# A message-passing layer on one core: another order inside each step, node blocks in smaller parts, and a later, longer shrinking of the pipeline's lags

## The chip, the core and the metric

The kernel runs on one core of a Trainium2 chip. Time is device microseconds of one execution. The kernel before took 2609.36 us (median of three executions, 2591.1 to 2622.12). The engines are called by the profile's names: PE (TensorE, matrix products), ACT (ScalarE), DVE (VectorE), POOL (GpSimd, which here only issues gathers) and SP (SyncE, which here only issues plain transfers).

## What is computed

A graph has 12,500 nodes with 64 features (`x`) and 200,000 edges, sorted by destination. Cut to what matters:

```python
nodes = x[edges].reshape(E, 128)                       # source row and destination row
gates = (ssp(edge_attr @ We1 + be1) @ We2 + be2) * soft_cutoff(edge_weight1)
h = ssp(nodes @ Wn1 + bn1) @ Wn2 + bn2
messages = h * gates                                   # E x 64
message_sum = zeros_like(x).at[dst].add(messages)
new = x + ssp(message_sum @ Ws1 + bs1) @ Ws2 + bs2
out = layernorm(x + new)                               # over the 64 features, no scale or shift
```

`ssp(v)` is `log(1 + exp(v)) - log 2`, and `soft_cutoff(d)` is `1 - sigmoid(5 (d - 3.5))`. All data are float32.

## The kernel before

**Groups.** The edges are worked on in 391 groups of 512, each as four columns of 128 (`K = 4`). Because edges are sorted by destination, the 256 edges of each half of a group go to destinations in a window of 42 neighbouring nodes (`W`); what would fall outside is dealt with after the loop in a branch that these data don't take.

**A group's chain**, with the lines of the profile:

- `gather` (L176, POOL): four indirect transfers fetch the source rows into `xg`, 128 rows each. They are issued 19 groups ahead (`AHEAD = 20`); `xg` has 25 buffers. In every 32nd group one of the four is fetched row by row through SP instead (`fetch`, L191, `xr`).
- `load` (L197, L204, SP): the edge attributes `eT` and two windows of a table of destination rows that are already multiplied by their part of `Wn1` (`wns`).
- `onehot` (L209, DVE): a one-hot of each edge's place in its window, beside the source row in `xg`.
- `transposes` (L217, PE, into a `tx` bank) and `xcopy` (L222, ACT, to `xT`): source rows and one-hots turned, so that one product with `wns` gives source part plus destination part.
- `layer1_edge` (L226, L228) and `layer1_node` (L233): first layers of the edge and node networks into one PSUM tile `z` of two banks. The edge part fills half of the first bank, the node part the other half and half of the second.
- `exps` (L243), `logs` (L246) on ACT and `softplus` (L251) on DVE: the activation, to `s`.
- `layer2_edge` (L257, L260) and `layer2_node` (L265) into `gh`.
- `hcut` (L270) and `message` (L274) on DVE: times the cutoff, and times the gates.
- `scatter` (L278, PE): messages times one-hots, that is, the sums over the window ("Sums' product"). It goes into the free half of the second bank of `z`, or into a `tx` bank in the last groups.
- `window` (L287, DVE): adds the two halves' 64 x 42 sums to `sums` at a place read from a register, which is loaded ahead of each of them.

PSUM holds eight banks: two `z` tiles of two banks, two of `gh`, two of `tx`.

**Order.** Nothing is planned by a scheduler. The code inside `tc.manual_schedule()` is the order on every engine, and each engine works through its instructions in that order, with waits on semaphores for what it needs from others. Step `i` of the loop works on different groups at once: layer 1 of group `i + 1`, layer 2 of `i - 1`, Sums' product of `i - 3`, transposes of `i + 3`. On PE a step is: Sums, layer 2 of the edges, layer 1, transposes, layer 2 of the nodes. On DVE: softplus, windows, h, message, one-hot. From step `both = last - CATCH_UP` on (`CATCH_UP = 12`, `last = 390`) the lags are shorter: layer 2 of `i`, Sums of `i - 1`, transposes of `i + 2`; the step in between does two groups of layer 2, the next one three of Sums.

**Node blocks.** When the sums of a block of 512 nodes are complete, the last network and the layer norm of this block are done inside the loop (`node_block`), in five parts, one in each following step: product with `Ws1` (L306) and clamping (L314, L315); logarithm on ACT (L318, L319) and softplus (L322); second product (L327, L330), doubling of `x` and centring (L334 to L337); square (L341) and variance (L345); root (L350, L351), scaling (L356 to L359) and store (L360). The block's rows of `x` (`y`, L312) are loaded in the first part. `block_steps` fixes after which group a block counts as complete. The last two blocks have 256 nodes each (`HE`); they are done after the last group, interleaved with each other. A part with a product takes a `tx` bank.

**Before the loop** constants, indices and the table of destination rows are prepared, among them `ws2` and the row of biases `brow`, which is cut into three bfloat16 pieces that a product adds up again.

Of the kernel before, what the change touches and what calls it, by code (L numbers as in the profile page):

```python
# [31 lines left out]

# [19 lines left out]

P = 128
D = 64
HE = 256
# [9 lines left out]
CATCH_UP = 12  # L65
# [7 lines left out]
def node_blocks(N):  # L73

    rest = N - NB
    first = rest % NB
    assert rest > 0 and first % 2 == 0 and first <= HE
    sizes = ([first] if first else []) + [NB] * (rest // NB) + [HE, HE]
    return [(sum(sizes[:i]), n) for i, n in enumerate(sizes)]
# [18 lines left out]
def gnn_resnorm_kernel(ctx: ExitStack, tc: tile.TileContext, a: dict, out: bass.AP, E: int):  # L98
# [52 lines left out]
    half = const.tile([P, 1], F32, name="half")  # L151
    ones3 = const.tile([PIECES, HE], BF16, name="ones3")
# [78 lines left out]
    def layer1_node(g, h):  # L231
        zn = zs[g][:, h, HE * (1 - h) : HE * (2 - h)]
        nc.tensor.matmul(zn, wns[:, g % REST, h, :], xTs[g][:, h], start=True, stop=True, skip_group_check=True)  # L233
# [29 lines left out]
    def layer2_node(g, h):  # L263
        for t in range(2):
            nc.tensor.matmul(ghs[g][:, 1, 2 * t + h, :], ss[g][:, 1 + h, t, :], wn2, start=False,  # L265
                             stop=h == 1 and t == 1, skip_group_check=True)
# [14 lines left out]

    def window(g):
        for h in range(2):
            base = nc.values_load(base_i[0:1, 2 * g + h : 2 * g + h + 1], engines=[DVE], min_val=0, max_val=N - 1,
                                  skip_runtime_bounds_check_because="it was clamped to these bounds")
            part = sums[h * D : (h + 1) * D, bass.ds(base, W)]
            nc.vector.tensor_add(part, part, scs[g][h * D : (h + 1) * D, h * W : (h + 1) * W])  # L287

    def node_block(first, n, pool):
# [7 lines left out]
        def tile3(name):  # L297
            return pool.tile([P, 2, 2, D], F32, name=name, bufs=2)[:p, :nq]
# [11 lines left out]
        def clamp():  # L310
            t["y"] = tile3("y")
            nc.sync.dma_start(t["y"], x[rows, :].rearrange("(q p k) d -> p q k d", q=nq, k=2))  # L312
            t["l"], t["zb"] = (pool.tile([P, HE], F32, name=name, bufs=2) for name in ("l_s", "zb"))
# [19 lines left out]
        def center():  # L333
            nc.vector.scalar_tensor_tensor(t["y"], t["y"], 2.0, t["u"][:, :nq], OP.mult, OP.add)  # L334
            mean = small("mean")
            nc.vector.tensor_reduce(mean, t["y"], AX.X, OP.add)
            nc.vector.scalar_tensor_tensor(t["y"], mean.to_broadcast([p, nq, 2, D]), -1.0 / D, t["y"], OP.mult, OP.add)  # L337
# [5 lines left out]
        def variance():  # L343
            t["v"] = small("var")
            nc.vector.tensor_reduce(t["v"], t["y2"], AX.X, OP.add)  # L345
            nc.vector.tensor_scalar(t["v"], t["v"], 1.0 / D, EPS, OP.mult, OP.add)

        def root():
            t["r"] = small("rstd")
            nc.scalar.activation(t["r"], t["v"], AF.Ln)  # L350
            nc.scalar.activation(t["r"], t["r"], AF.Exp, scale=-0.5)  # L351

        def store():

            v, r = t["v"], t["r"]
# [3 lines left out]
            nc.vector.tensor_mul(t["y"], t["y"], r.to_broadcast([p, nq, 2, D]))  # L359
            nc.sync.dma_start(out[rows, :].rearrange("(q p k) d -> p q k d", q=nq, k=2), t["y"])  # L360

        def then(f, g):
            def both():
                f()
                g()
            return both

        return [(hidden, clamp), (None, then(logs, ssp)), (layer2, center), (None, then(square, variance)),
                (None, then(root, store))]

    def node_part(part):
        if part[0]:
            part[0](tx_tile())
        part[1]()

    with tc.manual_schedule():
# [4 lines left out]
        with tc.tile_pool(name="prep", bufs=1) as prep:  # L381
# [23 lines left out]
            nc.vector.memset(half, 0.5)  # L405
            nc.vector.memset(ones3, 1.0)
# [40 lines left out]
            nc.vector.tensor_add(brow[:, 1:3, :], brow[:, 1:3, :], ps[:1, : 2 * D].rearrange("o (i d) -> o i d", d=D))  # L447
# [293 lines left out]
```

## Time and profile before

| | |
|---|---|
| median of three executions | 2609.36 us |
| the profiled execution | 1999.2 us, of which span 1997.4 us |
| mean granted clock of TensorE in it | 0.986 |
| busy: PE / weight loads / POOL | 1881.8 / 1505.4 / 1474.1 us |
| busy: DVE / ACT | 1050.5 / 919.0 us |
| first and last gather issued | 3.3 / 1950.2 us |
| moved by DMA | 143.15 MB, mean 72 GB/s |

The profiled execution is shorter than the three timed ones. Everything that is read from the trace belongs to this one execution. In the profile "idle before, releaser" is the time that an engine stood still ahead of an instruction and what ended it; "issue" means that nothing in the trace was waited for. A float32 product is recorded as two matmuls.

### The profile page before, as it was taken

To read this page: it belongs to the slowest core of one execution; us is meant where nothing else is said; L and a number is where in the kernel's file an instruction comes from. 1 tells how busy PE (TensorE), PEld (TensorE's weight loads), DVE (VectorE), ACT (ScalarE), POOL (GpSimd) and SP (SyncE) were. 2 spreads that over 40 slices of the span, in tenths; PEclk is the share of its full clock that TensorE was granted. 3 is DMA by queue.
4 is the path that set the end of the run, shared out by engine and by line. 5 is a ranking of instruction groups with operands and counts; after the bars stand their busy time and mean duration, and the time that the engine had idled before them with its cause. 6 is when DMAs were issued, how large, how long until landed. Compare 5 with 4: busy or idle time off the path is not lost.

```text
span 1997.4 us, 42101 instructions
## 1 busy us (share of the span) xinstructions
PE 1881.8 (94%) x11378; PEld 1505.4 (75%) x11378; DVE 1050.5 (53%) x2752; ACT 919.0 (46%) x1322; POOL 1474.1 (74%) x1555
## 2 busy tenths in 40 slices
PE   4999999999999999999999999999999999999996
PEld 4888888887777777777777777777777877777775
DVE  4455555555544545545555555555554555555555
ACT  1344545454444444444444444444454554444433
POOL 7777777777777777777777777777777777777770
PEclk9999999999999999999999999999998999999988
DMA  8432222222223223232222322232222232223220
GB/s 231 140 68 68 66 69 68 67 67 69 66 68 69 58 66 69 62 70 61 63 68 64 69 65 64 68 69 69 68 65 68 64 71 68 68 71 68 68 61 25
DMA packets 171021, 143.15 MB, mean 72 GB/s; under 512 B 46507, under 2 KB 142947, under 8 KB 170778
## 3 DMA queue, kind: packets, MB, share of 16 engines
q1 hardware_dynamic: 119778, 87.95, 15.2%
q0 software_dynamic: 49632, 50.92, 14.2%
q8 instruction: 95, 1.56, 0.3%
q10 hardware_dynamic: 1368, 1.51, 0.3%
q14 instruction: 148, 1.21, 0.2%
HBM read 130.57 MB, written 9.63 MB: 70 GB/s over the span
## 4 chain that ended last, share of the span: by engine, by line
PE 58%; DMA 20%; POOL 7%; issue 6%; ACT 4%; DVE 3%; DVEq 1%; POOLq 0%; SPq 0%; ACTq 0%
DMA xg<-in_x,src_i 19%; PE gh L265 11%; PE z L233 9%; PE gh L260 8%; PE z L228 8%; POOL xg L176 7%; PE tx L217 6%; PE z L278 6%; PE gh L257 4%; PE z L226 3%; ACT u L246 2%; ACT u L243 2%; PE z L471 2%; DVE s L251 1%; DVE sums L287 1%
## 5 line engine op out<-in xcount | busy, mean ns | idle before, releaser
L176 POOL DMA_INDIRECT xg<-in_x,src_i x1551 | 1473.9, 950 | 476.8 <-issue 310.0
L251 DVE SCALAR_TENSOR_TENSOR s<-u,z 128x768 f32<-128x768 f32 x392 | 373.2, 952 | 842.6 <-ACT u L246 776.7
L243 ACT ACTIVATE u<-z 128x768 f32<-128x768 f32 x392 | 317.4, 810 | 975.8 <-PE z L233 975.8
L233 PE MATMUL z<-xT,wns 106*128 106x256 f32 x1564 | 410.0, 384 | 0.0
L265 PE MATMUL gh<-consts,s 128*128 128x64 f32 x3128 | 394.1, 269 | 0.0
L265 PEld LDWEIGHTS gh<-consts,s 128*128 128x128 f32 x3128 | 391.6, 196 | 0.1
L246 ACT ACTIVATE u<-u,one 128x768 f32<-128x768 f32 x392 | 366.1, 934 | 12.3
L217 PE MATMUL tx<-consts,xg 128*106 128x128 f32 x1552 | 283.5, 283 | 69.9 <-DMA xg<-in_x,src_i 63.9
L233 PEld LDWEIGHTS z<-xT,wns 106*128 106x128 f32 x1564 | 301.3, 193 | 44.4 <-issue 0.4
L217 PEld LDWEIGHTS tx<-consts,xg 128*106 128x106 f32 x1552 | 194.9, 133 | 164.9 <-DMA xg<-in_x,src_i 116.1
L260 PE MATMUL gh<-consts,s 128*128 128x128 f32 x1564 | 279.9, 301 | 0.0
L228 PE MATMUL z<-eT,consts 128*128 128x256 f32 x782 | 277.9, 437 | 0.0
L260 PEld LDWEIGHTS gh<-consts,s 128*128 128x128 f32 x1564 | 205.1, 191 | 89.0 <-issue 88.3
L278 PE MATMUL z<-xg,msg 128*128 128x84 f32 x1500 | 235.4, 279 | 0.0
L222 ACT COPY xT<-tx 106x512 f32<-106x512 f32 x391 | 221.6, 567 | 9.5 <-PE tx L217 9.1
L278 PEld LDWEIGHTS z<-xg,msg 128*128 128x128 f32 x1500 | 198.1, 192 | 0.0
L270 DVE TENSOR_TENSOR h<-gh,cut 128x256 f32<-128x256 f32 x391 | 166.0, 425 | 14.7 <-PE gh L265 2.2
L274 DVE TENSOR_TENSOR msg<-gh,h 128x256 f32<-128x256 f32 x391 | 166.0, 425 | 13.5
L228 PEld LDWEIGHTS z<-eT,consts 128*128 128x128 f32 x782 | 118.0, 190 | 47.6 <-issue 1.5
L287 DVE TENSOR_TENSOR sums<-sums,z 64x42 f32 x750 | 144.3, 192 | 13.0 <-issue 6.1
L257 PE MATMUL gh<-row,ones 3*128 3x512 bf16 x391 | 150.8, 386 | 0.0
L209 DVE TENSOR_TENSOR xg<-consts,rel 128x168 f32<-128x168 f32 x391 | 126.8, 325 | 1.1 <-issue 0.4
(79 smaller groups left out, 590.9 us busy)
## 6 DMA issues: line engine op xcount, KB each, us to landing
eT<-in_eT SPq DMA_DIRECT2D x391, 128.0 KB
xg<-in_x,src_i POOLq DMA_INDIRECT x1551
xr<-in_x SPq DMA_DIRECT2D x1536, 0.2 KB
wns<-table SPq DMA_DIRECT2D x782, 21.0 KB
table<-tb SPq DMA_DIRECT2D x14, 448.0 KB
sums<-in_xT SPq DMA_DIRECT2D x7, 455.0 KB
y<-in_x SPq DMA_DIRECT2D x23, 128.0 KB
out<-y SPq DMA_DIRECT2D x23, 128.0 KB
```

Of the source, the lines that this page charges most:

```text
L176: nc.gpsimd.indirect_dma_start(out=xg[:, k, :D], out_offset=None, in_=x, in_offset=bass.IndirectOffsetOnAxis(ap=src_i[:, g, k : k + 1], ax ...
L217: nc.tensor.transpose(tx[:, k, :], row, ident)
L222: nc.scalar.copy(xT, xTs[g])
L228: nc.tensor.matmul(zs[g][:, 0, :HE], we1.rearrange("a h d -> a (h d)"), eTs[g], start=False, stop=True, skip_group_check=True)
L233: nc.tensor.matmul(zn, wns[:, g % REST, h, :], xTs[g][:, h], start=True, stop=True, skip_group_check=True)
L243: nc.scalar.activation(us[g][:, part], z_of(g)[:, part], AF.Exp)
L246: nc.scalar.activation(us[g][:, part], us[g][:, part], AF.Ln, bias=one)
L251: nc.vector.scalar_tensor_tensor(ss[g].rearrange("p i t e -> p (i t e)")[:, part], us[g][:, part], BIG, z_of(g)[:, part], OP.min, OP.max)
L257: nc.tensor.matmul(gh, ones3[:, :P], row3.rearrange("q i k d -> q (i k d)"), start=True, stop=False, skip_group_check=True)
L260: nc.tensor.matmul(v[:, 0, t], ss[g][:, 0, t, :], we2, start=False, stop=False, skip_group_check=True)
L265: nc.tensor.matmul(ghs[g][:, 1, 2 * t + h, :], ss[g][:, 1 + h, t, :], wn2, start=False, stop=h == 1 and t == 1, skip_group_check=True)
L278: nc.tensor.matmul(sc, msgs[g][:, 2 * t : 2 * t + 2, :].rearrange("p h f -> p (h f)"), xgs[g][:, 2 * t : 2 * t + 2, D:DW], start=t == 0, s ...
```

## The change

- **Order in a step.** On PE: layer 2 of the edges, layer 1 of the edges, a node block's product if there is one, layer 1 of the nodes, then Sums' product into the same `z` tile, transposes, layer 2 of the nodes. Sums' product goes into `z` in all but the last groups, so that `tx` is left to transposes and node blocks. On DVE: h, message, windows, one-hot, softplus, node parts. The two window places of a group are loaded into registers at once.
- **Node blocks.** A block has eleven parts (`Part`). The load of `y` is issued when five more groups are missing (`PREPARE`), the other ten parts stand in the steps `BLOCK_STEPS` after completion, up to the twelfth; towards the end in three steps (`BRIEFLY`). The columns of `ws2` and of the bias are centred beforehand, so `y` alone is centred, and this before the second product. The constant of the root comes in as a bias (`eps`). The last block is one of 512 nodes.
- **Lags.** From `ends = last - 14` on Sums are two groups behind instead of three; transposes go from three groups ahead to two and then to one, each time after a step without transposes, and then stand first in a step. Layer 2's lag stays. The last group and what is still behind it is written out after the loop, with the windows' places loaded ahead.

The diff, cut to its core:

```diff
-CATCH_UP = 12
+CATCH_UP = 14
+PREPARE = 5
+BLOCK_STEPS = (1, 2, 3, 3, 4, 5, 6, 7, 8, 12)
+BRIEFLY = (1, 1, 1, 1, 2, 2, 2, 3, 3, 3)
...
-    rest = N - NB
-    first = rest % NB
-    sizes = ([first] if first else []) + [NB] * (rest // NB) + [HE, HE]
+    first = N % NB
+    sizes = ([first] if first else []) + [NB] * (N // NB)
...
+    def window_bases(g):
+        _, window_at[g] = nc.values_load_multi_w_load_instructions(
+            base_i[0:1, 2 * g : 2 * g + 2], engines=[DVE], min_val=0, max_val=N - 1,
...
-        return [(hidden, clamp), (None, then(logs, ssp)), (layer2, center), (None, then(square, variance)),
-                (None, then(root, store))]
+        return [Part(None, fetch), Part(hidden, clamp), Part(None, logs), Part(None, center), Part(None, ssp),
+                Part(layer2, add), Part(None, square), Part(None, variance), Part(None, root), Part(None, scale),
+                Part(None, store)]
...
+            nc.vector.tensor_reduce(mean[:, :2], ws2, AX.X, OP.add)
+            nc.vector.tensor_reduce(mean[:1, 2:], brow[:, 3, :], AX.X, OP.add)
+            nc.vector.scalar_tensor_tensor(ws2, mean[:, :2].to_broadcast([P, 2, D]), -1.0 / D, ws2, OP.mult, OP.add)
+            nc.vector.scalar_tensor_tensor(brow[:, 3, :], mean[:1, 2:].to_broadcast([1, D]), -1.0 / D, brow[:, 3, :],
...
+                groups = [i - 3] if i < ends else [i - 3, i - 2] if i == ends else [i - 2]
                 third[i] = [g for g in groups if g >= 0]
+                ahead[i] = [i + 3] if i < ends else [i + 2] if i == ends + 1 else [i + 1] if i > ends + 2 else []
...
+            for i in range(-3, last - 1):
+                now = parts.pop(i, [])
                 at(load, i + LOADS)
                 fetch(i)
                 if i > 0:
                     at(gather, i + AHEAD - 1)
+                early = i > ends
+                if early:
+                    for g in ahead[i]:
+                        transposes(g)
+                        xcopy(g)
+                at(layer2_edge, i - 1)
+                if i >= -1:
                     zs[i + 1] = z_tile()
+                    layer1_edge(i + 1)
+                    for part in now:
+                        if part.tensor:
+                            part.tensor(tx_tile())
+                    layer1_node(i + 1)
+                for n, g in enumerate(third[i]):
+                    scatter(g, zs[i + 1][:, 1, HE + 2 * W * n : HE + 2 * W * (n + 1)])
+                at(exps, i + 1)
+                at(logs, i + 1)
+                if not early:
+                    for g in ahead[i]:
+                        transposes(g)
+                        xcopy(g)
+                at(layer2_node, i - 1)
+                at(hcut, i - 1)
+                at(message, i - 1)
+                for g in third[i]:
                     window(g)
                 for g in ahead[i]:
                     at(onehot, g + 2)
+                at(softplus, i + 1)
+                for part in now:
+                    part.others()
...
+            begun.pop(2).others()
+            transposes(last)
+            xcopy(last)
+            layer2_edge(last - 2)
+            zs[last] = z_tile()
+            layer1_edge(last)
+            layer1_node(last)
+            for some in (edge, node):
+                exps(last, some)
+                logs(last, some)
+            for g in range(last - 3, last + 1):
+                window_bases(g)
+            softplus(last, edge)
+            layer2_node(last - 2)
+            scatter(last - 3, tx_tile()[:, : 2 * W])
...
+            scatter(last, tx_tile()[:, : 2 * W])
+            window(last)
+            for part in begun:
+                node_part(part)
```

## The prediction

> **What bounds the kernel now.** I read the page's busy line and the gather's row first, then the waits, then busy time by stage, and last the timeline of the steady stretch, of the turn into the end phase and of the end.
>
> ```profile
> PE 1881.8 (94%) x11378; PEld 1505.4 (75%) x11378; DVE 1050.5 (53%) x2752; ACT 919.0 (46%) x1322; POOL 1474.1 (74%) x1555
> L176 POOL DMA_INDIRECT xg<-in_x,src_i x1551 | 1473.9, 950 | 476.8 <-issue 310.0
> ```
>
> POOL looks less loaded than PE, but each of its 1551 gathers costs 0.95 us and then 0.30 us before the next: 1.25 x 1551 = 1939 us from 3.3 us on, so the last starts at 1950.2. A group of four gathers takes 5.0 us.
>
> ```profile
> PEld tx L217 <- DMA xg<-in_x,src_i: 116.1, 209, 1.5
> PE tx L217 <- DMA xg<-in_x,src_i: 63.9, 155, 1.3
> ```
> ```profile
> 200.00:400.00 200.00, 199.98 (x1272) 164.86 (x1271) 109.44 (x284) 101.48 (x142) 151.50 (x160) 1.00 0.29 68
> 1000.00:1200.00 200.00, 190.19 (x1156) 150.44 (x1155) 102.57 (x272) 93.67 (x133) 151.25 (x160) 0.99 0.29 67
> ```
>
> Columns: length, then busy time and count of PE, weight loads, DVE, ACT, POOL, then granted clock. Until about 400 us PE lives on the twenty groups gathered ahead and never idles; later its rate falls by 1156/1272 although it isn't slower: its transposes wait for gathers. So from 400 us POOL sets the pace, and PE has 5.0 - 4.41 = 0.6 us a group to spare. The 4.41 is the distance of two L233 (299.69 and 304.10 us) and splits by the starts between them: transposes L217 0.44, L265 0.84, L278 0.55, L257 0.32, L260 0.65, L226 0.20, L228 0.54, L233 0.87.
>
> The end is different.
>
> ```profile
> 1920.00:1925.00 5.00, 5.00 (x17) 3.25 (x17) 2.19 (x7) 1.25 (x2) 3.78 (x4) 0.54 0.27 66
> 1925.00:1930.00 5.00, 5.00 (x21) 4.45 (x21) 2.61 (x7) 1.79 (x4) 3.77 (x4) 0.50 0.29 61
> ```
> ```profile
> 1918.28 0.65 PE L278 MATMUL tx<-xg,msg 128*128 128x84 f32 x4 [0.92 <-DVE sums L287]
> 1919.85 0.65 PE L278 MATMUL tx<-xg,msg 128*128 128x84 f32 x4 [0.92 <-DVE sums L287]
> 1950.19 0.94 POOL L176 DMA_INDIRECT xg<-in_x,src_i  x1 [0.30 <-DMA xg<-in_x,src_i]
> 1968.77 0.62 PE L217 MATMUL tx<-consts,xg 128*106 128x128 f32 x4 [0.22 <-PE z L233]
> 1971.02 1.03 PE L233 MATMUL z<-xT,wns 106*128 106x256 f32 x4
> 1983.10 0.20 DVE L287 TENSOR_TENSOR sums<-sums,tx 64x42 f32 x1 [0.36 <-DVE sums L287]
> 1992.07 0.29 DVE L359 TENSOR_TENSOR y<-y,rstd 128x128 f32<-128x128 f32 x1
> ```
>
> At the turn (step 378) PE computes one second layer and two Sums products extra and twice stands 0.92 us, because three products share two tx banks. Then it runs at half clock for some 14 us. It ends 16 us behind POOL: the last gather lands near 1952.7, but the last group's transposes start at 1968.8. From there it is one chain: first layer to 1972.05, last window 1983.3, last scaling 1992.4, the store's 5.0 us, 1997.4.
>
> **What the Trainium skill says.** "TensorE: Matmul & The Clock Gate", Part 1 (the HAM clock gate): an idle window of about 3.4 us puts TensorE at half clock. The trace shows half clock with much shorter stalls ahead: after 0.17 and 0.63 us of gather waits at 1531 to 1533 us the clock is 0.50 until 1548.5, and again after the turn above. "DMA: Bandwidth & Descriptors", Anatomy of one DMA: a transfer costs some 2 us fixed, mostly the write receipt; here the chain has 2.46 us from a gather's issue to its landing. "PSUM — Partial Sum Buffer", Terms: two engines must not be on one bank at once. That is why, in the built order, the exponential now waits for the Sums product that stands behind layer 1 in its tile; no timing of it is in this trace.
>
> **The change part by part.** *Sums product behind layer 1, every group.* The counts of PE, ACT and POOL instructions per group stay. PE's order becomes L257, L260, L226, L228, L233, Sums, transposes, L265: the same terms, 4.41 us. Whether a neighbour hides more or less of a weight load isn't shown; between -0.02 and +0.02 us a group, I take 0. The exponential starts 0.55 us later, and DVE now does h, message, windows, one-hot and only then the softplus. Counted from the end of L233: Sums 0.55, transposes 0.44, L265 0.84 and its drain 0.17 give 2.0; DVE adds 0.42 + 0.45 + 0.42 + 0.33 + 0.95, so the softplus ends at 4.6. ACT's two passes end at about 2.5, earlier. L260 wants that softplus a group later, at 4.41 + 1.83 + 0.32 = 6.56. Cover 1.95 us: cost 0. Behind the waiting exponential stand only the logarithm and the xT copy, wanted two groups later.
>
> *Node blocks over twelve steps.* The same twelve DVE instructions for a block, in eleven parts (the input's load first); a step carries at most about 1.3 us (L336 0.42 + L337 0.43 + L322 0.42), which fits in the 1.95. In the trace of before, the blocks' waits on PE are small: L330 on l_s 6.6 + 3.7 us, L306 on Sums 3.4, most of it in the end phase. While POOL leads, a PE stall of 0.6 us is free anyway. Worth 0 to 6 us, I take 0 outside the end. On SP, y's load moves five groups earlier and the store waits for a scaling done four steps before, so neither blocks the loads behind them. The two blocks of 256 become one of 512.
>
> *Preparation.* Four small DVE instructions and a memset, about 1 us by L336 and L337 (0.29 each at 128x128). DVE waits 7.4 us for the distances there: 0, at most +1.
>
> *Lags shrink over 14 groups.* Layer 2's lag stays; transposes go from three groups ahead to one in two steps without transposes, Sums from three to two in one step. Follow PE: the transposes of step 375 end a wait near 1892.6. Step 376 without transposes but with two Sums products puts the next at 1898.4, 0.8 behind the gather; the next omission puts them at 1906.8, 4.2 behind. Ten groups at 0.6 us spare win this back, less the PE work of two blocks, (1.03 + 0.74) x 2 = 3.5 us. So the last transposes start 0 to 7 us after the landing (7 if half clock comes again), I take 2: 1954.7 instead of 1968.8.
>
> *The last groups.* From transposes to the end of layer 1: 0.45 + 0.75 + 0.73 + 0.97 = 2.9 us (before 3.2), 1957.6. Then layer 2 of two groups (0.97 + 0.86 and a wait each), h, message (0.9), the last product (0.6), windows whose register loads (0.36 each) were made ahead: by the same rows 7.5 us against 11.3: 1965.1. The last block: product about 1.5, clamp to softplus 1.97, second layer 1.3, add, square, variance, root 0.5 each, scaling 0.95: 7.8 us, then the store's 5.0. The centring is gone from it (0.29 + 0.32) but 512 rows cost 0.42 where 256 cost 0.29. Before, window to end took 14.1, now 12.8. End: 1977.9, so -19.5 us of the profiled 1997.4 (that execution's time is 1999.2, 1.8 more).
>
> **From there to the median.** The median is 2609.36, 610 us above the profiled time, and the trace doesn't show why. Spread over 391 groups that is some 6.4 us a group, either a PE 1.45 times slower or a gather of 1.6 us. If PE is slow, gathers lead to the end and there is no waiting for them: what is saved is the two stalls (1.8), the shorter chain (3.8 or a little more) and the block (1.3), about 7 us. If gathers are slow, PE wins its arrears back before the end in both kernels: 5 us and what is left of the 14. So 5 to 19.5, I take 12: 2597.4.
>
> **Rivals.** (a) *The gap to the median is half clock, and stalls start it.* A stretch of 13.7 us at 8.2 instead of 4.41 us a group loses 6.3 us of PE; some 97 would make 610. If the spread blocks prevent seven, that is -44: 2565. For it: both stretches follow stalls. Against: PE at half clock builds a stock of gathered groups, so stalls end, and only two are seen.
> (b) *Slower: the softplus, now last on DVE, comes too late for L260.* It decides from 1.95 us of delay on DVE (register loads of 0.36 us exposed for every window, plus a part of 1.3). With 24 blocks of ten steps, 240 steps at 0.2 us: +48, so 2657, if PE leads in the timed runs; under POOL's lead the 0.6 us swallow it. For it: DVE was idle 842 us ahead of the softplus and the change spends that slack. Against: the count above.
> (c) *The gain stays inside the noise or is lost*: the end starved to one group ahead lets PE idle, half clock returns, the last chain runs at 0.5 (its PE share, some 8 us, doubles): -19.5 + 7 + 8 = -4.5, so 2605.
>
> **How the numbers follow.** A change of less than 1% (26 us) can hardly be told from none: the three runs alone spread over 31 us. Forecast 0.53, (c) 0.12, (a) 0.24, (b) 0.11. Faster by over 1% is (a) and the forecast's lower edge with the spread of the runs, 0.09: 0.33. Slower is (b) with a little spread: 0.12. Rest 0.55. The range reaches to (a) and halfway to (b), leaving out 0.2: 2564 to 2625; the likeliest case's own is 2583 to 2609.
>
> **What would show it.** Right: 1.25 us a gather and its last start near 1950 unchanged; 4.41 us between L233 at 300 us; the last transposes within 7 us of the last landing; no 0.92 us waits of Sums on windows; span 1974 to 1986. Wrong: waits of L260 on the softplus, a busy PE with more than 4.45 us a group in the first 400 us, or last transposes still over 10 us late. The largest doubt is the timed state, of which I have no trace.

## The result, and the profile after

The changed kernel takes 2596.18 us (median of 20 executions, 2583.43 to 2611.70); the kernel before, run beside it, 2598.33 (2579.37 to 2622.43). The ratio is estimated as 1.0018, with a 95% interval of 0.9994 to 1.0041 (the quotient of the two medians is 0.9992): no difference that can be measured. This program runs in one of two conditions, each of which held through whole sets of runs, and in which the kernel before takes 2580 to 2600 us (four sets) or some 1998 us (the execution whose profile the prediction read, and the last set of runs below), so a time is compared only with times of its own condition.

The profile of the changed kernel is of the longer condition, so that, unlike the one the prediction had, it shows what the timed runs do: 2583.43 us, of which span 2581.7, at a mean clock of 0.843. Lines have moved against the kernel before: gathers are L184 (before: L176), transposes L225, layer 1 L234, L236 and L242, the exponential L253, the logarithm L256, the softplus L261, layer 2 L267, L270 and L276, h L281, messages L285, and the Sums product L289. From its page, the busy line, the clock in 40 slices, and groups of instructions (busy, mean ns of one, idle time before them and what ended most of it):

```profile
PE 2139.4 (83%) x11373; PEld 1756.0 (68%) x11373; DVE 1113.9 (43%) x2745; ACT 919.4 (36%) x1317; POOL 1473.2 (57%) x1555
PEclk9968888888888788888888878888888888888886
...
L184 POOL DMA_INDIRECT xg<-in_x,src_i x1551 | 1473.0, 950 | 958.5 <-issue 364.2
L253 ACT ACTIVATE u<-z 128x768 f32<-128x768 f32 x392 | 317.0, 809 | 1494.7 <-PE z L289 501.5
...
L270 PE MATMUL gh<-consts,s 128*128 128x128 f32 x1564 | 308.2, 324 | 181.4 <-DVE s L261 150.1
```

A gather still takes 0.95 us, but POOL stands 958.5 us instead of 476.8. TensorE is 83% busy and no other engine over 57%: nothing is full. The idle time sits where results of PE are handed on. The exponential (L253) waits 501.5 us for the Sums product (L289), and L270 waits 150.1 us for the softplus. By stretch (length, then busy time and count of PE, weight loads, DVE, ACT, POOL, clock, DMA share, GB/s):

```profile
200.00:400.00 200.00, 171.03 (x908) 140.01 (x907) 81.65 (x195) 71.27 (x97) 120.49 (x129) 0.83 0.22 51
1000.00:1200.00 200.00, 171.61 (x914) 141.10 (x915) 86.21 (x210) 74.71 (x104) 123.32 (x131) 0.85 0.23 54
```

There is no first phase any more in which PE never idles: 908 matmul records in 200 us from the start on, where the profile before had 1272 and later 1156. From layer 1 of group 20 to that of group 376 a group takes 6.21 us; it was 4.86.

What happens inside one step is read in the timeline, here POOL, ACT and PE one after the other (start, duration, engine, line, and in brackets the idle time before and its releaser):

```profile
1002.31 0.94 POOL L184 DMA_INDIRECT xg<-in_x,src_i  x1 [1.37 <-PE tx L225]
1003.56 0.94 POOL L184 DMA_INDIRECT xg<-in_x,src_i  x1 [0.31 <-issue]
1004.81 0.95 POOL L184 DMA_INDIRECT xg<-in_x,src_i  x1 [0.30 <-issue]
1006.06 0.94 POOL L184 DMA_INDIRECT xg<-in_x,src_i  x1 [0.30 <-issue]
1008.39 0.94 POOL L184 DMA_INDIRECT xg<-in_x,src_i  x1 [1.38 <-PE z L236]
...
1002.08 0.81 ACT L253 ACTIVATE u<-z 128x768 f32<-128x768 f32 x1 [3.80 <-PE z L289]
1008.15 0.81 ACT L253 ACTIVATE u<-z 128x768 f32<-128x768 f32 x1 [3.83 <-PE z L236]
...
1001.53 0.57 PE L289 MATMUL z<-xg,msg 128*128 128x84 f32 x4
1001.94 0.60 PE L225 MATMUL tx<-consts,xg 128*106 128x128 f32 x4
1002.38 1.00 PE L276 MATMUL gh<-consts,s 128*128 128x64 f32 x8
1005.32 1.23 PE L270 MATMUL gh<-consts,s 128*128 128x128 f32 x4 [1.63 <-DVE s L261]
```

The Sums product of 1001.53 ends at 1002.10, but the exponential that waits for it starts at 1008.15, 6 us later. In the profile before, the exponential (L243) started 0.04 us after the end of the matmul that it waits for in every one of 391 cases, as here (1003.76 + 1.03 = 1004.79, then 1004.83):

```profile
1003.76 1.03 PE L233 MATMUL z<-xT,wns 106*128 106x256 f32 x4
1004.83 0.81 ACT L243 ACTIVATE u<-z 128x768 f32<-128x768 f32 x1 [2.15 <-PE z L233]
```

In the profile after, the median is 3.7 us from the end of the Sums product, for which it waits now (4.4 us from the end of layer 1). The trace also keeps when PE's completion counter was raised, the semaphore by which the other engines learn that a product is done. Beside the gathers' starts (rounded to 0.01 us):

```
gathers start       1002.31   1003.56   1004.81   1006.06                                        1008.39
completions of PE        1003.66   1004.41   1005.19   1006.63   1008.13 .16 .20 .23 .26   1008.36
```

Six completions, by their order those of L289, of four transposes and of L276, appear within 0.23 us, 2.1 us after the start of the last gather of a row of four, and then the other engines start: ACT at 1008.15, DVE at 1008.38, POOL at 1008.39. Over the middle 60% of the profile a completion comes at 0.69 per us in the 1.25 us that follow a gather's start, and at 18 per us between 2.00 and 2.25 us after a gather that has no successor yet. In the profile before it is 2.0 per us in the 1.25 us after a gather's start. "Perfetto Trace Analysis" of the Trainium skill, section Tensor Engine Instruction (MATMUL, LD_WEIGHTS), says that a matmul's end in a profile is an estimate, and that the semaphore goes up only when PSUM has acknowledged the writes. That gap, 0.04 us in the profile before, is what grew to 6 us in the step shown here; what it was spent on isn't in the trace.

The end of the gathers and of the span:

```profile
2400.00:2450.00 50.00, 42.85 (x253) 35.06 (x251) 25.15 (x64) 21.22 (x32) 19.06 (x20) 0.90 0.20 51
2500.00:2550.00 50.00, 47.33 (x249) 37.80 (x248) 24.42 (x62) 21.60 (x33) 0.00 (x0) 0.81 0.10 29
```
```profile
2549.36 1.06 PE L225 MATMUL tx<-consts,xg 128*106 128x128 f32 x4
2553.38 1.91 PE L242 MATMUL z<-xT,wns 106*128 106x256 f32 x4
2555.33 0.38 ACT L253 ACTIVATE u<-z 128x256 f32<-128x256 f32 x1 [4.28 <-PE z L242]
```

The last gather starts at 2431.0, the last transposes at 2549.4: the last transposes start 118 us after the last gather and not 19, as in the profile before (1950.19 and 1968.77), since POOL keeps its 19 to 20 groups of lead to the last. And with no gather about, the exponential starts 0.04 us after its matmul again (2553.38 + 1.91 = 2555.29, then 2555.33).

### The profile page after: what moved, and what is told of

The parts are those of the page before. It is cut to its first block, busy times and chain, and to the rows that moved or that the text cites. A ratio compares the mean times of both kernels' runs of the same rounds, so it can differ in the third digit from the quotient of the medians.

```text
span 2581.7 us, 40774 instructions
## 1 busy us (share of the span) xinstructions
PE 2139.4 (83%) x11373; PEld 1756.0 (68%) x11373; DVE 1113.9 (43%) x2745; ACT 919.4 (36%) x1317; POOL 1473.2 (57%) x1555
## 4 chain that ended last, share of the span: by engine, by line
PE 69%; DVE 17%; issue 8%; another core or an unknown queue 3%; DVEq 2%; ACT 1%; DMA 1%; ACTq 0%; SPq 0%
PE z L242 15%; PE z L236 11%; PE gh L270 11%; PE gh L276 9%; PE z L289 7%; DVE s L261 6%; PE tx L225 6%; PE z L234 4%; DVE msg L285 3%; DVE h L281 3%; PE gh L267 3%; DVE xg L217 2%; PE tx L324 2%; DVE sums L305 1%
## 5 line engine op out<-in xcount | busy, mean ns | idle before, releaser
L184 POOL DMA_INDIRECT xg<-in_x,src_i x1551 | 1473.0, 950 | 958.5 <-issue 364.2
L253 ACT ACTIVATE u<-z 128x768 f32<-128x768 f32 x392 | 317.0, 809 | 1494.7 <-PE z L289 501.5
L281 DVE TENSOR_TENSOR h<-gh,cut 128x256 f32<-128x256 f32 x391 | 165.8, 424 | 1166.8 <-PE z L236 292.4
L242 PE MATMUL z<-xT,wns 106*128 106x256 f32 x1564 | 504.9, 454 | 7.9 <-issue 4.7
L270 PE MATMUL gh<-consts,s 128*128 128x128 f32 x1564 | 308.2, 324 | 181.4 <-DVE s L261 150.1
L276 PE MATMUL gh<-consts,s 128*128 128x64 f32 x3128 | 433.7, 285 | 20.0 <-issue 20.0
L276 PEld LDWEIGHTS gh<-consts,s 128*128 128x128 f32 x3128 | 426.9, 211 | 22.4 <-issue 22.3
L270 PEld LDWEIGHTS gh<-consts,s 128*128 128x128 f32 x1564 | 227.0, 209 | 287.6 <-DVE s L261 196.2
L242 PEld LDWEIGHTS z<-xT,wns 106*128 106x128 f32 x1564 | 360.2, 232 | 75.4 <-issue 5.6
L261 DVE SCALAR_TENSOR_TENSOR s<-u,z 128x768 f32<-128x768 f32 x392 | 373.2, 952 | 50.3 <-issue 26.9
L256 ACT ACTIVATE u<-u,one 128x768 f32<-128x768 f32 x392 | 365.9, 933 | 12.7
L236 PE MATMUL z<-eT,consts 128*128 128x256 f32 x782 | 311.3, 484 | 0.1
L289 PEld LDWEIGHTS z<-xg,msg 128*128 128x128 f32 x1548 | 286.7, 231 | 35.9 <-issue 1.1
L225 PE MATMUL tx<-consts,xg 128*106 128x128 f32 x1552 | 274.3, 306 | 4.1 <-DVE xg L217 2.7
L289 PE MATMUL z<-xg,msg 128*128 128x84 f32 x1548 | 266.2, 301 | 1.2 <-issue 0.2
L225 PEld LDWEIGHTS tx<-consts,xg 128*106 128x106 f32 x1552 | 214.5, 162 | 7.7 <-DVE xg L217 3.0
L285 DVE TENSOR_TENSOR msg<-gh,h 128x256 f32<-128x256 f32 x391 | 165.8, 424 | 13.4
L236 PEld LDWEIGHTS z<-eT,consts 128*128 128x128 f32 x782 | 131.0, 210 | 53.8 <-issue 14.0
L267 PE MATMUL gh<-row,ones 3*128 3x512 bf16 x391 | 155.2, 397 | 11.2 <-DVE msg L285 4.8
```

Of the source, the lines that this page charges most:

```text
L184: nc.gpsimd.indirect_dma_start(out=xg[:, k, :D], out_offset=None, in_=x, in_offset=bass.IndirectOffsetOnAxis(ap=src_i[:, g, k : k + 1], ax ...
L225: nc.tensor.transpose(tx[:, k, :], row, ident)
L236: nc.tensor.matmul(zs[g][:, 0, :HE], we1.rearrange("a h d -> a (h d)"), eTs[g], start=False, stop=True, skip_group_check=True)
L253: nc.scalar.activation(us[g][:, part], z_of(g)[:, part], AF.Exp)
L256: nc.scalar.activation(us[g][:, part], us[g][:, part], AF.Ln, bias=one)
L261: nc.vector.scalar_tensor_tensor(ss[g].rearrange("p i t e -> p (i t e)")[:, part], us[g][:, part], BIG, z_of(g)[:, part], OP.min, OP.max)
```

## The experiments

Ratios are to the kernel before in the same set of runs, with 95% intervals; the changed kernel's own is 1.0018 (0.9994 to 1.0041). Times by group are from one profiled execution each.

**Is it the change, or is the kernel before like that too?** The kernel before, nothing edited.

> The kernel before, profiled once more. In the profile of the changed kernel TensorE's completions reach the other engines late: the exponential starts a median of some 4.4 us after the last matmul of layer 1. Theory (the late completions belong to the chip's state and not to the change): this profile is as long as the timed executions, 2570 to 2625 us, POOL is about 57% busy, the exponential waits for layer 1 (some 400 to 500 us in sum), L260 waits for the softplus (100 us or more), and the last transposes start 100 us or more after the last gather. Rival (the change made TensorE wait, and the kernel before is slow for another reason): gathers of 1.6 us or matmuls 1.45 times as long in the records, and L260 waits less than 20 us for the softplus.

2594.39 us (ratio 0.9991, 0.9937 to 1.0044). Its profile is of an execution of 2621.06 us, the longest of seven, where the changed kernel's is of the shortest of twenty; so their lengths are not to be compared:

```profile
PE 2245.3 (86%) x11378; PEld 1778.2 (68%) x11378; DVE 1047.0 (40%) x2752; ACT 918.6 (35%) x1322; POOL 1473.1 (56%) x1555
L176 POOL DMA_INDIRECT xg<-in_x,src_i x1551 | 1472.9, 950 | 1005.9 <-issue 377.5
L243 ACT ACTIVATE u<-z 128x768 f32<-128x768 f32 x392 | 317.3, 810 | 1458.6 <-PE z L233 629.2
```

In the main the theory holds: same gather, POOL at 56%, an exponential that waits 629.2 us (400 to 500 were expected), last gather at 2478.3 and last transposes at 2589.9. The wait of L260 for the softplus was wrong: it is 20.6 us and not 100 or more, and PE stands in other places. The exponential's delay, too, is less here than in the changed kernel: from the end of its layer 1 to its start the median is 0.8 us, the longest 24. The 622 us between the two profiles of one kernel split into 36 us before the first layer 1 (113.6 instead of 77.5), 53 in the first 20 groups, 525 in the next 356 (6.34 instead of 4.86 us) and 6 after that.

**What sets the pace of the longer condition?** One piece of work is taken from PE, one from ACT, one from POOL.

```diff
 # without the node half of layer 2
-                at(layer2_node, i - 1)
 # without the logarithm
-                at(logs, i + 1)
 # two gathers
-        for k in range(K - (g in by_rows)):
+        for k in range(2):
...
-            row = ... else xgs[g][:, k, :DW]
+            row = ... else xgs[g][:, k % 2, :DW]
```

> The changed kernel without the node half of layer 2 (L276, eight matmul records of a group; the messages are then wrong). It takes TensorE work away that lies outside the loop of layer 1, exponential, logarithm, softplus and L270. Theory A (TensorE itself is slow in its timed state: completions come at a rate of one 256-column layer-1 product per 0.75 us, and the sum of such times is the period of 6.2 us a group): a share of 0.7 us a group goes, some 270 us, so 2300 to 2380 us. Theory B (the completions are only late, and the loop's latency of exponential, logarithm and softplus sets the period): within 40 us of the changed kernel's 2596. Theory C (gathers set the pace): no change.

> The changed kernel without the logarithm of every group (L256, 0.93 us of ACT; the softplus is then wrong). It shortens the loop by 0.93 us and takes nothing from TensorE. Theory A (TensorE's own rate): within 40 us of 2596. Theory B (loop latency): 0.45 to 0.93 us a group, so 180 to 360 us less, 2240 to 2420 us. Theory C (gathers): no change.

> The changed kernel with two gathers of a group instead of four; the transposes of columns 2 and 3 read columns 0 and 1 (the output is then wrong). TensorE's work is the same. Theories A and B: within 20 us of 2596, since gathers run ahead anyway. Theory C (gathers of 1.6 us set the pace in the timed executions): 500 us less or more.

Without L276: 2695.03 us, ratio 1.0396 (1.0282 to 1.0510), *slower* by 4% with eight matmul records a group less, which none of the three theories had. Without the logarithm: 2594.57, ratio 1.0023 (0.9985 to 1.0062), nothing. With two gathers: 2028.88, ratio 0.7827 (0.7754 to 0.7899), 568 us less. Theories A (PE's own rate) and B (the loop's latency) both fall. C comes nearest, with two of its three numbers, though POOL is only 57% busy and a gather takes 0.95 us as ever. The profile with two gathers shows what had changed beside POOL (the page's busy line, then the timeline of PE and ACT):

```profile
PE 1926.4 (95%) x11373; PEld 1601.2 (79%) x11373; DVE 1115.4 (55%) x2744; ACT 919.4 (45%) x1317; POOL 739.7 (37%) x786
```
```profile
1002.51 0.57 PE L289 MATMUL z<-xg,msg 128*128 128x84 f32 x4
...
1003.12 0.81 ACT L253 ACTIVATE u<-z 128x768 f32<-128x768 f32 x1 [2.10 <-PE z L289]
```

1002.51 + 0.57 = 1003.08: the exponential is 0.04 us behind again, h too (median 0.037 us), PE is 95% busy, and the step shown takes 4.35 us (the next L289 starts at 1006.86); the mean from group 20 to 376 is 4.83. This in runs between which the kernel before took 2597. So the number of gathers decides over 568 us, and not by their time on POOL alone, which is 5.0 of 6.2 us a group: with half of them PE's completions are prompt again.

**Gathers, waits for gathers, or rows?** The same transposes as with two gathers, but all four issued; and four gathers of half the rows.

```diff
 # four issued, two read
-            row = ... else xgs[g][:, k, :DW]
+            row = ... else xgs[g][:, k % 2, :DW]
 # half the rows
-                out=xg[:, k, :D], ... ap=src_i[:, g, k : k + 1]
+                out=xg[:D, k, :D], ... ap=src_i[:D, g, k : k + 1]
```

> The changed kernel with its four gathers, but the transposes of columns 2 and 3 read columns 0 and 1, so that nothing on TensorE waits for the gathers of two columns (the output is then wrong). It has the transposes of the kernel with two gathers, which took 2029 us. Theory (gathers themselves, four in a row on POOL, hold TensorE's completions back): 2560 to 2620 us and an exponential that starts some 4 us after layer 1. Rival (TensorE's own waits for the gathers' semaphores do it): 2000 to 2100 us.

> The changed kernel with four gathers of 64 rows instead of 128: as many instructions, half the rows and bytes (the output is then wrong; the other half is zeroed once in each of the 25 buffers). If it is the rows that are fetched that hold TensorE's completions back: 2000 to 2100 us, as with two gathers. If it is the gather instructions on POOL, each with 0.95 and 0.30 us: 2500 to 2620 us.

Four issued, two read: 2733.86 us, ratio 1.0588 (1.0509 to 1.0668), above the theory's range and far above the rival's. Half the rows: 2575.31, ratio 0.9985 (0.9951 to 1.0020). It isn't PE's waiting for the gathers' semaphores, and hardly the rows or bytes; it is the number of gather instructions, or something that each of them brings whatever its rows: with half the rows a gather still takes 0.91 us on POOL, and the next one starts 1.21 us after it. Why the first of the two is slower than the changed kernel isn't explained.

**Spacing and number.** The four gathers in two pairs, the second behind a memset of `xg[:, 2, :1]` that stands after the softplus on DVE; and three gathers.

```diff
 # pairs
-                    at(gather, i + AHEAD - 1)
+                    at(gather, i + AHEAD - 1, False, range(0, 2))
...
                 at(softplus, i + 1)
+                if i > 0:
+                    at(gather, i + AHEAD - 1, False, range(2, K), 2)
 # three
-        for k in range(K - (g in by_rows)):
+        for k in range(3):
...
-            row = ... else xgs[g][:, k, :DW]
+            row = ... else xgs[g][:, k % 3, :DW]
```

> The changed kernel, all of its work done, with the four gathers of a step split: columns 0 and 1 at the start as before, columns 2 and 3 behind a one-column memset of VectorE after the softplus of the step. With two gathers a group, pairs with 2.16 us between them, TensorE's completions were prompt. Theory (completions get out where POOL pauses, so a pause in the middle of the four lets half of them out earlier): a group of 5.2 to 5.9 us instead of 6.2, 2150 to 2480 us. Rival (what counts is the number of gathers, not their spacing): 2560 to 2640 us.

> The changed kernel with three gathers of a group; the transposes of column 3 read column 0 (the output is then wrong). Theory (POOL's loop sets the period: the gathers of a group, and then a pause of some 1.2 us until TensorE's held completions come out and free the next buffer): 391 times 1.25 us less than 2596, so 2080 to 2150 us, with two gathers then bound by TensorE at 2029. Rival (a threshold between three and four: with three gathers completions are prompt): 2020 to 2040 us. Rival (a threshold between two and three): 2500 to 2620 us.

Pairs: 2957.90 us, ratio 1.1456 (1.1379 to 1.1534), above the theory's range and the rival's. Three: 2174.85, ratio 0.8441 (0.8383 to 0.8499), 25 us above the theory's range and far from both rivals'. POOL's timeline with pairs (its line numbers are 5 higher), and its wait from the list of waits (in all, times, longest):

```profile
1004.29 0.95 POOL L189 DMA_INDIRECT xg<-in_x,src_i  x1 [0.30 <-issue]
1010.21 0.95 POOL L189 DMA_INDIRECT xg<-in_x,src_i  x1 [4.97 <-DVE xg L180]
1011.46 0.95 POOL L189 DMA_INDIRECT xg<-in_x,src_i  x1 [0.30 <-issue]
...
1018.96 0.95 POOL L189 DMA_INDIRECT xg<-in_x,src_i  x1 [0.31 <-issue]
1024.86 0.95 POOL L189 DMA_INDIRECT xg<-in_x,src_i  x1 [4.95 <-DVE xg L180]
```
```profile
POOL xg L189 <- DVE xg L180: 832.9, 196, 9.4
```

The edit did not part the gathers into pairs. From 1010.21 to 1018.96 eight of them follow one another at 1.25 us, and then POOL stands 4.95 us for the memset. Over the whole profile there are 143 rows of eight and 57 of four, and after a row of eight the next gather comes 4.6 us (median) later than the usual 1.25. So this run doesn't say whether a pause within a group lets completions out earlier; with POOL made to wait for a later point of the step, the softplus, its rows and its pauses became longer.

In the changed kernel's profile nearly all rows, 343, are of four gathers, and after one the next gather comes 1.07 us (median) later than the usual 1.25. So a group is a row of *n* gathers at 1.25 us and a pause: with four gathers 6.21 us, on the mean 5.0 + 1.21; with three 5.19, 3.75 + 1.44; with the edit meant for pairs 7.26, 5.0 + 2.26, mostly one long pause for two groups. These pauses are what is left of the measured times; a fixed pause of 1.2 us, the theory's, gives the time with three gathers to 25 us and that with pairs not at all. With two gathers and such a pause the sum, 3.7, lies below the step of 4.35 us that PE needs there, and PE sets the pace.

I read this as the loop of the timed runs: POOL waits for the Sums product that frees its buffer of 25 groups ago; that completion is held until POOL's last gather is through; so POOL, by waiting, ends its own wait. It fits that 0.93 us less on ACT and eight matmul records less didn't help. That the latter cost 4%, and two columns left unread 6%, it doesn't give. In the profiles of both, rows of eight are frequent (108 and 60, against 5 in the changed kernel's); whether they are a cause or a consequence isn't shown, and no run tests the loop by a change to it alone.

**The parts of the change.** The softplus ahead of h again, shorter lags over 6 groups only, and blocks in five consecutive steps.

```diff
 # softplus first
+                at(softplus, i + 1)
                 at(layer2_node, i - 1)
                 at(hcut, i - 1)
...
-                at(softplus, i + 1)
 # lags
-CATCH_UP = 14
+CATCH_UP = 6
 # blocks
-BLOCK_STEPS = (1, 2, 3, 3, 4, 5, 6, 7, 8, 12)
+BLOCK_STEPS = (1, 2, 2, 2, 3, 4, 4, 5, 5, 5)
```

> The changed kernel with the softplus ahead of h, messages, windows and one-hot on VectorE. Prediction's step (the softplus at the end costs nothing): no gain, 2590 to 2625 us, perhaps slower because h then stands behind a softplus that waits for the late exponential. Rival (b) of the prediction (the late softplus holds L270 and eats the end's gain): 10 to 50 us faster, 2545 to 2587 us.

> The changed kernel with CATCH_UP 6 instead of 14: the lags shrink over the last 6 groups alone. In the trace of the changed kernel, which is in the timed state, the stretch from layer 1 of group 360 to that of group 390 takes 185.5 us, in that of the kernel before 173.7, and with two gathers (2026 us in all) 187: with a shorter lag and no gathers to wait for, TensorE stands for its own results. Theory (in the timed state the shorter lags are a loss, which cancels the shorter last chain): 5 to 20 us faster than the changed kernel, ratio to the kernel before 0.994 to 1.000. Prediction's step (shrinking early saves what the end is behind the gathers): 3 to 12 us slower than the changed kernel, ratio 1.003 to 1.007.

> The changed kernel with the parts of a node block in five consecutive steps, as before the change, instead of twelve. Prediction's step (the spreading is worth 0 to 6 us in the middle): 2590 to 2605 us, ratio to the kernel before 0.999 to 1.005. Rival (a) of the prediction (stalls of the blocks start half clock, and spreading prevents them): 20 to 45 us slower than the changed kernel, ratio 1.01 to 1.02.

Softplus first: 2708.44, ratio 1.0467 (1.0391 to 1.0542). Its list of waits, and two of PE's groups (idle time last):

```profile
DVE s L261 <- ACT u L256: 820.9, 240, 6.2
```
```profile
L270 PE MATMUL gh<-consts,s 128*128 128x128 f32 x1564 | 314.7, 330 | 9.3 <-DVE s L261 9.3
L267 PE MATMUL gh<-row,ones 3*128 3x512 bf16 x391 | 163.1, 417 | 107.9 <-DVE msg L285 68.6 <-DVE h L281 25.4 <-PE gh L276 7.5
```

L270 no longer waits for the softplus (9.3 us instead of 181.4), but h stands behind a softplus that waits for a late exponential, so messages are late and L267 waits instead. In this condition, and given the new order of PE, the softplus belongs last. Rival (b) had the right wait and the wrong cause.

Lags over 6 groups: 2589.63, ratio 1.0014 (0.9976 to 1.0053), the same as over 14 as far as this can tell; it lies between my two theories and bears out neither. Blocks in five steps: 2636.33, ratio 1.0121 (1.0030 to 1.0212), from only four executions of 2589 to 2652. In the new order the spreading may be worth some 1%, more than the 0 to 6 us of my step; the number is rival (a)'s. Its mechanism is not shown by that. In this profile, of the slowest of the four, a pause of POOL, from the start of the last gather before it to the next start, takes a mean 2.9 us, against 2.6 in the changed kernel's, with nearly the same median (2.29 and 2.32): a few long pauses more, and 45 rows of eight instead of 5.

**Sums first again**, the last run, to see whether the new place of the product takes back what the spreading gives.

```diff
+                if i >= -1:
+                    zs[i + 1] = z_tile()
+                for n, g in enumerate(third[i]):
+                    scatter(g, zs[i + 1][:, 1, HE + 2 * W * n : HE + 2 * W * (n + 1)])
                 at(layer2_edge, i - 1)
                 if i >= -1:
-                    zs[i + 1] = z_tile()
                     layer1_edge(i + 1)
...
                     layer1_node(i + 1)
-                for n, g in enumerate(third[i]):
-                    scatter(g, zs[i + 1][:, 1, HE + 2 * W * n : HE + 2 * W * (n + 1)])
```

> The changed kernel with the Sums product at the head of a step again, ahead of L270, where the kernel before had it; spread blocks and shorter lags stay. Undoing the spread alone cost 1.2% (0.3 to 2.1), undoing the shorter lags nothing, and yet both kernels take the same time. Theory (the product's place behind layer 1 costs what the spread gains: the exponential then waits for one more completion of TensorE, and the buffer of POOL comes free later in the step): 0.5 to 1.5% faster than the changed kernel, ratio to the kernel before 0.987 to 0.997. Rival (the place is worth nothing, or is what makes the spread worth while: its completion comes out together with those of the transposes and of the node half of layer 2): 1.000 to 1.04.

2036.21 us against 1997.74 for the kernel before (11 executions, 1993.11 to 2007.45), ratio 1.0203 (1.0171 to 1.0234). This set fell in the shorter condition, on the chip on which the kernel before had taken 2597 earlier, so it doesn't answer the question it was meant for. It answers another: in the condition whose profile the prediction argued from, all of the change but the product's place *loses* 38 us. Its profile (PE's timeline, DVE's timeline, then stretches as above) shows a stall that the profile before has not, here at one of 24 blocks:

```profile
990.75 0.28 PE L352 MATMUL tx<-rs,ones 3*128 3x256 bf16 x1
992.73 1.23 PE L355 MATMUL tx<-consts,l_s 128*128 128x128 f32 x4 [1.70 <-DVE l_s L347]
993.74 1.91 PE L242 MATMUL z<-xT,wns 106*128 106x256 f32 x4
```
```profile
990.60 0.95 DVE L261 SCALAR_TENSOR_TENSOR s<-u,z 128x768 f32<-128x768 f32 x1
991.47 0.41 DVE L334 TENSOR_REDUCE mean<-y 128x4 f32<-128x256 f32 x1
991.91 0.42 DVE L335 SCALAR_TENSOR_TENSOR y<-mean,y 128x256 f32<-128x256 f32 x1
992.25 0.42 DVE L347 SCALAR_TENSOR_TENSOR l_s<-zb,l_s 128x256 f32<-128x256 f32 x1
```
```profile
985.00:990.00 5.00, 5.00 (x33) 4.11 (x33) 2.99 (x10) 3.21 (x6) 3.78 (x4) 1.00 0.30 69
990.00:995.00 5.00, 3.31 (x11) 2.42 (x11) 2.57 (x6) 0.00 (x0) 3.77 (x4) 0.73 0.24 53
995.00:1000.00 5.00, 5.00 (x21) 4.17 (x20) 1.45 (x5) 2.22 (x3) 3.78 (x4) 0.50 0.17 35
1000.00:1005.00 5.00, 5.00 (x18) 3.89 (x17) 1.41 (x3) 1.07 (x2) 3.78 (x4) 0.50 0.24 60
```

The block's softplus L347 comes after the group's softplus and the centring on DVE, and the block's second product L355 stands early in the next step on PE, between the two halves of layer 1. PE stands 1.70 us, and is at half clock for over 10 us after it. The waits' list has this wait 24 times:

```profile
PE tx L355 <- DVE l_s L347: 39.2, 24, 1.9
```

In the profile before the same wait (L330 for L322) comes to 3.7 us in 5 times. Not each of the 24 costs as much. By the clock in the trace, of the 22 stalls up to group 376, all of 1.4 to 1.9 us, nine are followed by half clock for 10 to 20 us, eight by half clock for 3.4 us, and five by none. Up to there POOL's pace hides most of this (4.90 us a group instead of 4.86, 14 us in all). Then the block that is done in three steps does it again inside the shrinking lags, and PE doesn't recover (DVE's zb and l_s are awaited, then stretches of 20 us):

```profile
1930.32 0.26 PE L352 MATMUL tx<-rs,ones 3*128 3x256 bf16 x1 [1.08 <-DVE zb L340]
1931.44 1.22 PE L355 MATMUL tx<-consts,l_s 128*128 128x128 f32 x4 [0.86 <-DVE l_s L347]
```
```profile
1930.00:1950.00 20.00, 18.49 (x62) 14.27 (x62) 8.15 (x23) 6.67 (x12) 15.12 (x17) 0.53 0.14 30
1950.00:1970.00 20.00, 19.57 (x67) 15.29 (x67) 5.06 (x12) 5.68 (x8) 0.82 (x1) 0.50 0.25 66
1970.00:1990.00 20.00, 18.94 (x75) 14.29 (x75) 7.73 (x19) 5.88 (x8) 0.00 (x0) 0.61 0.02 5
```

Layer 1 of groups 376 to 390 spans 101.6 us; in the profile before 77.6. The last transposes start at 2006.3, 56 us after the last gather. That all of the 38 us come from this stall and the half clock behind it is read from the trace; no run takes the stall out alone.

## Why the prediction was right, point by point

The number was right, 2597.4 for 2596.18, and so was the likeliest class. Most of the reasons behind the 12 us that it took off were not: the interval, -1.6 to +10.7 us, leaves no room for a saving of 5 to 19.5, and 2597.4 fits because the median of the kernel before, measured again, is itself 2598.33, 11 us below the 2609.36 of the first three executions that I started from. That is luck: the 12 us taken off happen to meet the 11 us by which those three were high.

- *(i) POOL sets the pace, PE has 0.6 us to spare.* True of the profile read, and not of the timed runs. There a group takes 6.2 us, of which POOL's gathers are 5.0, and the rest, as I read it, is its wait for PE's held completions. The step on the transfer to the median offered "either a PE 1.45 times slower or a gather of 1.6 us". The second is near as a rate (6.21/4 = 1.55), but it isn't a longer gather: 0.95 + 0.30 as ever, and a pause after each four. (Of the sum in that step, 1939 us from 3.3 on end at 1942 and not at 1950.2: the gathers' mean distance is 1.253 us, and POOL pauses six times in the first 52 us.)
- *"If gathers are slow, PE wins its arrears back before the end."* This is the step that failed. The pace of POOL's loop does not make the end wait for gathers: POOL stays some 20 groups ahead, ends 118 us early, and the stretch that the change shortens on paper has no gather in it. From layer 1 of group 376 the two profiles of the longer condition have 86.9 + 28.3 us (changed) and 83.3 + 27.1 (before), one execution each: 4.8 longer, instead of 5 to 19.5 shorter.
- *Softplus last on DVE, cover 1.95 us, cost 0.* Right that it does no harm: put first, it costs 4.5% more. The cover itself went: L270 waits 150.1 us, and its weight loads too, for a softplus that is late because its exponential is.
- *Node blocks, 0 to 6 us.* Mis-sized, in both directions by condition: spread over twelve steps they may save some 1% in the longer condition (0.3 to 2.1, of four executions); for the shorter one I looked at how much DVE time a step carries and not at what PE waits for, the block's softplus, now last of all. That stall, 24 times 1.6 us and behind most of them a stretch of half clock, is in none of my sums. The changed kernel has the same order of blocks, and with two gathers the same waits (49.3 us at L355, 24 times); itself it wasn't run in the shorter condition.
- *Preparation, 0 to +1.* Right: first layer 1 at 111.9 us (before 113.6), and 76.9 against 77.5 in the shorter condition.
- *Lags, last transposes 2 us after the last landing.* Wrong in both: 118 and 56 us after the last gather's start. "No 0.92 us waits of Sums" is right; L289 idles 1.2 us over all groups. Lags shrinking over 14 or over 6 groups make no difference that these runs can tell.
- *Last chain, 23.2 us from the last transposes to the end.* Measured 32.3 in the changed kernel, 29.4 and 28.7 before, and 27.7 with Sums first: half clock in it, which rival (c) had priced at 8.
- *Rivals.* (c), the gain stays inside the noise, comes nearest, by its result and by half clock at the end. (a)'s mechanism, stalls of blocks that start half clock, is real, but in the shorter condition the new order makes such stalls instead of preventing them. (b)'s wait is there in the longer condition, with another cause.

What stays open: what in the hardware holds the completions while gathers run, why the same kernel on the same chip is free of it in other runs, whether the recording of the trace itself has a part in it, and where the 1% of the spread blocks, if there is one, is lost again in the changed kernel. A version that beats both kernels didn't come out of this: none of the runs that do all the work is faster than either.

## What to carry to other kernels

Ask first whether the profiled execution is a sample of the timed ones: 1999 against 2609 us meant that every wait in the profile belonged to another run than the ones to be predicted, and no edit to a stage could be priced until there was a profile of the longer kind. When no engine is full and work taken off PE or ACT gains nothing, look at the time from the end of a producer to the start of its consumer, and for what sits in the same stretch on an engine that has no data in common with them. And when a part is moved "last" on an engine, follow the consumer of each thing that now stands behind it, not only the load of the step.

## What was unexpected in the hardware

- In the longer condition PE's completions reach other engines late while gathers run on POOL: 0.69 per us in the 1.25 us after a gather's start, and bursts, mostly of six at 0.034 us from each other, 2.0 to 2.25 us after the last start. In the profile before gathers stand in the same row, in its middle 60% without a single pause, and completions come at 2.0 per us. "Perfetto Trace Analysis" of the Trainium skill, section DMA Instruction — SWDGE (GPSIMD), says that a gather's recorded end is that of writing its descriptors and not of moving data. It fits that the burst comes about 1.1 us after the recorded end of 0.95 us; that it is the data movement which holds the completions is not shown.
- The other counters' records differ too. Of the increments that the program's instructions make, the profile before has records of 3910 of 3967 for PE, 1313 of 1320 for ACT and 24177 of 24816 for the landing gathers (16 each); the profile after has 3661 of 3950, 765 of 1315 and 6305 of 24816. Whether the missing ones were merged or only not recorded isn't shown, and rates of completions are of those on record.
- SP is slowed too. A move between registers takes 29 ns in the profile before, with four exceptions in 2320 (up to 42 ns); in the profile after the mean is 92 ns and 6% take over 0.6 us.
- Less work made it slower: without the eight matmul records of L276 a group went from 6.21 to 6.58 us, and the clock fell to 0.72.
- Half clock after short stalls, but not after each: with Sums first, one 1.7 us stall of PE (991.0 to 992.7) is followed by more than 10 us at 0.50, and like ones by 20 us, 3.4 us or none. The page "TensorE: Matmul & The Clock Gate" of the Trainium skill, Part 1, gives an idle window of about 3.4 us as what leads to half clock; here it came behind stalls of half that length in 17 of 22 cases.
